# Channel order between two convolutions, chosen so that seven copies of all partitions replace 28 copies of 32

## The chip, the cores and the metric

The program runs on one core of one Trainium2 chip. Its time is the device time of one execution in microseconds (us). Five engines work beside each other: TensorE (PE, its weight loads PEld), VectorE (DVE), ScalarE (ACT), GpSimd (POOL), and SyncE (SP), which here does little but issue DMA copies. Each has a queue of its own that is worked off in order; they wait for each other by semaphores. SBUF has 128 partitions; a tile is written here as partitions x elements.

## The reference

Layer 0 is a residual block of 32 parallel bottleneck paths (P=32, D=4, C=256) over eight images of 56 x 56 x 256; layer 1 is a linear attention and a mixture of eight experts, top two, on the same 25,088 tokens.

```python
def _path(x, w1, b1, g1, be1, m1, v1, w2, b2, g2, be2, m2, v2, w3, b3, g3, be3, m3, v3):
    h = jnp.einsum('nhwc,cd->nhwd', x, w1) + b1                 # 256 -> 4, conv1
    h = jax.nn.relu(_bn(h, g1, be1, m1, v1))
    h = conv_general_dilated(h, w2, (1, 1), 'SAME') + b2        # 3 x 3, 4 -> 4, conv2
    h = jax.nn.relu(_bn(h, g2, be2, m2, v2))
    h = jnp.einsum('nhwd,dc->nhwc', h, w3) + b3                 # 4 -> 256, conv3
    return jax.nn.relu(_bn(h, g3, be3, m3, v3))
x = relu(sum of the 32 paths + x)
t = x + attention(layernorm(x));  t = t + moe(layernorm(t))
```

The 32 paths of four channels make 128 rows, one for each SBUF partition, after conv1 and after conv2.

## The kernel before

The tokens are cut into S = 56 chunks of 448 (eight image rows). A loop over slots (L1462) works on several chunks at once: in slot s, conv3 of chunk s, conv1 of chunk s+2, the copies R and conv2 of chunk s+1, the end of chunk s-1 (store, head statistics), attention of chunk s-8, and the tiles of the experts that are known by then. The `places` table (L1402) gives every step a place between 0 and 1 in its slot, and `issue` (L1430) sorts the steps by it; so PE, ACT and DVE run in this written order. SP and POOL are not among the ordered engines (L72): the scheduler sets their order. Slots before attention starts use the places marked "alone".

The path of a chunk through the first layer:

- conv1 (`conv1_steps`, L240): 128 rows of products, scaled and put by ACT into `h1` (L263), a whole image of 58 x 58 with a border, 128 partitions.
- `spread_taps` (L274): conv2 needs, on partitions 32 dx to 32 dx + 31, the 32 rows of a group g shifted by dx = 0, 1, 2. So R is 96 x 4 x 580, and each of the 4 groups x 3 shifts is one DMA copy of 32 partitions, 12 in all (L284), on SP; for chunk 0 a third of them are on ACT's queue.
- conv2 (`conv2_steps`, L290): for each of three dy, four products, one for each group, with 96 x 32 weights `W2t` (L298); ACT makes `h2` (L307).
- `halves` (L310): DVE splits h2 into hi and lo (L315, L316). conv3 wants, on partitions 4i + v, row i of quarter ab, hi for even v and lo for odd v: `hl` is 128 x 4 x 448. Each of 4 quarters x 4 values of v is one copy of 32 partitions, 16 in all (L321); for chunk 0 half are on ACT's queue.
- conv3 (`pair`, L578): 32 steps of two products (L588), which use `hl[rows, ab, :]` with ab = step // 4 % 4; ACT takes the positive part of one (L593), DVE adds the other (L596), and `sum_paths` (L602) sums the four paths of a partition group on PE (L609).

A copy of SP waits, in the built program, for the copy issued eight before it (eight completion semaphores in turn), besides what it needs itself.

Before the loop stands the setup: loads of W1, bn1, bn2 (L92 to L97), twelve copies W2s on ACT's queue (L206), then conv1 of chunks 0 and 1 and R of chunk 0 (L332, L333), the g and bias copies (L177, two each on SP and ACT), `picks` (L345), which move W3 into `W3hl` through PE (L370 to L381), the bias tables (L384 to L404), conv2 of chunk 0 (L405), and the sums of the biases (L407).

Of the kernel before, what the change touches and what calls it, by code (L numbers as in the profile page):

```python
# [8 lines left out]
F32 = mybir.dt.float32  # L9
# [4 lines left out]
ALU = mybir.AluOpType  # L14
AX = mybir.AxisListType
# [10 lines left out]
def kernel(  # L26
# [24 lines left out]
    nc = tc.nc  # L51
    B, N, C = x.shape
    HW = 56
    NP = W3.shape[0]
    D = W3.shape[1]
# [3 lines left out]
    P = 128  # L59
    NF = C // P  # L60
# [5 lines left out]
    NG = P // 32  # L66
# [9 lines left out]
    const = ctx.enter_context(tc.tile_pool(name="const", bufs=1))  # L76
# [7 lines left out]
    def load(s):  # L84
        b, c = divmod(s, NCH)
        X = xin.tile([T, KT, C], F32, tag="xi", name=f"xi_{s}")
        nc.sync.dma_start(
            out=X, in_=x[b, c * CH : (c + 1) * CH, :].rearrange("(k q) c -> q k c", q=T)
        )
        xs_in[s] = X  # L90

    W1s = const.tile([P, NF, P], F32, name="W1s")  # L92
    nc.sync.dma_start(out=W1s, in_=W1.rearrange("(f c) m -> c f m", c=P))
    bn1s = const.tile([P, 5], F32, name="bn1s")
    nc.sync.dma_start(out=bn1s, in_=bn1)
    bn2s = const.tile([P, 5], F32, name="bn2s")
    nc.sync.dma_start(out=bn2s, in_=bn2)  # L97
    load(0)


    ident = const.tile([P, P], F32, name="ident")
# [45 lines left out]
    GP = NP // NG  # L147
    W2t = const.tile([3 * 32, NG, 3, 32], F32, name="W2t")
# [3 lines left out]
    NPL = 4  # L152
    NQ = NP // (2 * NPL)
# [3 lines left out]
    sumb = const.tile([P, NF, 1], F32, name="sumb")  # L157
# [1 line left out]
    nc.vector.tensor_reduce(  # L159
        gather, ident.rearrange("q (p c) -> q c p", c=32), AX.X, ALU.add  # L160
    )
    xtp = ctx.enter_context(tc.tile_pool(name="xtp", bufs=4))
    taps = ctx.enter_context(tc.tile_pool(name="taps", bufs=1))
    split = ctx.enter_context(tc.tile_pool(name="split", bufs=1))
    hlp = ctx.enter_context(tc.tile_pool(name="hlp", bufs=2))
    setup_pool = tc.tile_pool(name="setup", bufs=1)
    setup = setup_pool.__enter__()


    CQ = C // 4  # L170
# [28 lines left out]
    path32 = setup.tile([P, GP, D], F32, name="path32")  # L199
# [3 lines left out]
    W2s = setup.tile([3 * 32, NG, 3, D], F32, name="W2s")  # L203
    for dx in range(3):
        for g in range(NG):
            nc.scalar.dma_start(  # L206
                out=W2s[32 * dx : 32 * dx + 32, g],
                in_=W2[32 * g : 32 * g + 32].rearrange(
                    "q (dy dx o) -> dx q dy o", dy=3, dx=3
                )[dx],  # L210
            )
    for g in range(NG):
        for dy in range(3):
            nc.vector.tensor_tensor(
                W2t[:, g, dy, :].rearrange("q (p o) -> q p o", o=D),
                path32[: 3 * 32],
                W2s[:, g, dy, None, :].to_broadcast([3 * 32, GP, D]),
                ALU.mult,
            )

# [50 lines left out]
    TL = (ROWS + 2) * W58  # L271
    tapped = {}

    def spread_taps(s):  # L274

        b, c = divmod(s, NCH)
        R = taps.tile([3 * 32, NG, TL], F32, tag="R", name=f"R_{s}")
        flat = h1.rearrange("p r w -> p (r w)")
        r0 = c * ROWS * W58
        for g in range(NG):  # L280
            for dx in range(3):
                n = TL - dx
                queue = nc.scalar if s == 0 and dx == 1 else nc.sync
                queue.dma_start(  # L284
                    out=R[32 * dx : 32 * dx + 32, g, :n],
                    in_=flat[32 * g : 32 * g + 32, r0 + dx : r0 + dx + n],
                )
        tapped[s] = R

    def conv2_steps(s):  # L290
        ps = []

        def taps_of(dy):
            if dy == 0:
                ps.append(ps_mm.tile([P, 512], F32, tag="mm", name=f"c2_{s}"))
            R = tapped[s]
            for g in range(NG):
                nc.tensor.matmul(  # L298
                    ps[0][32 * g : 32 * g + 32, :CH],
                    W2t[:, g, dy, :],  # L300
                    R[:, g, :].rearrange("q (r w) -> q r w", w=W58)[:, dy : dy + ROWS, :HW],
                    start=(dy == 0), stop=(dy == 2),
                )
            if dy == 2:
                del tapped[s]
                h2 = split.tile([P, CH], F32, tag="h2", name=f"h2_{s}")
                nc.scalar.activation(h2, ps[0][:, :CH], AF.Relu, bias=sh2, scale=sc2)  # L307
                h2s[s] = h2

        def halves():  # L310

            h2 = h2s[s]
            hi = split.tile([P, CH], F32R, tag="hi", name=f"hi_{s}")
            lo = split.tile([P, CH], F32R, tag="lo", name=f"lo_{s}")
            nc.vector.tensor_copy(hi, h2)  # L315
            nc.vector.tensor_tensor(lo, h2, hi.bitcast(F32), ALU.subtract)  # L316
            hl = hlp.tile([P, NQ, CH], F32R, tag="hl", name=f"hl_{s}")
            for ab in range(NQ):
                for v, part in enumerate((hi, lo, hi, lo)):
                    queue = nc.scalar if s == 0 and v % 2 else nc.sync  # L320
                    queue.dma_start(  # L321
                        out=hl[v : P : 4, ab, :].bitcast(F32),
                        in_=part[32 * ab : 32 * ab + 32, :].bitcast(F32),
                    )
            h2s[s] = hl

        return [
            (0.8, lambda: taps_of(0)), (0.8, lambda: taps_of(1)), (0.8, lambda: taps_of(2)),
            (0.8, halves),
        ]  # L330

    all_of(conv1_steps(0), conv1_steps(1))  # L332
    spread_taps(0)  # L333


# [9 lines left out]
    picks = setup.tile([P, 2, NQ, P], F32, name="picks")  # L345
    nc.gpsimd.memset(picks, 0.0)
    for part in range(2):
        nc.vector.tensor_copy(
            picks[:, part].rearrange("q a (i v h) -> q (a i) v h", v=2, h=2)[:, :, part, :],
            ident[:, :, None].to_broadcast([P, P, 2]),  # L350
        )

    own = setup.tile([P, P // 16, 16], F32, name="own")
    group_mask(own, P // 16, 16, 1.0)
# [15 lines left out]
    for ab in range(NQ):  # L370
# [12 lines left out]

    pmod = setup.tile([NP, NPL], F32, name="pmod")  # L384
    nc.vector.tensor_reduce(
        pmod, ident[:NP, :NP].rearrange("q (g p) -> q p g", p=NPL), AX.X, ALU.add
    )
    pdiv = setup.tile([NP, NP // NPL], F32, name="pdiv")
    nc.vector.tensor_reduce(
        pdiv, ident[:NP, :NP].rearrange("q (g p) -> q g p", p=NPL), AX.X, ALU.add  # L390
    )
    b4 = setup.tile([NP, NCG, NPL, 32], F32, name="b4")
    for pl in range(NPL):
# [13 lines left out]
    for f in range(NF):  # L407
        tp = ps_mm.tile([P, 512], F32, tag="mm", name=f"tp_sb_{f}")
        nc.tensor.transpose(tp[:, :NP], bias3[:, f * P : (f + 1) * P], ident[:NP, :NP])
        b3T = setup.tile([P, NP], F32, name=f"b3T_{f}")  # L410
        nc.scalar.copy(b3T, tp[:, :NP])
        sub = setup.tile([P, NQ, NPL], F32, name=f"sub_{f}")
        nc.vector.tensor_copy(
            sub, b3T.rearrange("q (a r n) -> q a r n", r=2, n=NPL)[:, :, 1, :]
        )
        nc.vector.tensor_reduce(
            sumb[:, f, :], sub.rearrange("q a n -> q (a n)"), AX.X, ALU.add
        )
    setup_pool.__exit__(None, None, None)

    spill = ctx.enter_context(
# [116 lines left out]
    for e in range(M):  # L538
# [6 lines left out]
        out=below, in_=below, compare_op=ALU.is_ge, fill=0.0, base=-1,  # L545
# [8 lines left out]
        out=earlier, in_=earlier, compare_op=ALU.is_ge, fill=0.0, base=-1,  # L554
# [905 lines left out]
    r, upto = -1, -2  # L1460
    waiting, left = [], []
    for s in range(S + A + 1):  # L1462
        a = s - A
# [6 lines left out]
        if is_chunk(s + 1):  # L1470
            work_of.extend(at("taps" + era, [(0.0, lambda: spread_taps(s + 1))]))
            work_of.extend(at("conv2" + era, conv2_steps(s + 1)))
# [105 lines left out]
```

## Time and profile before

| | us |
|---|---|
| median of three runs | 3262.89 |
| lowest, highest | 3259.10, 3267.65 |
| the profiled execution | 3247.72 |
| its span | 3246.0 |
| PE busy | 2939.6 |
| DVE busy | 2222.5 |
| ACT busy | 1918.3 |
| POOL busy | 1900.8 |
| R copies, SP | 668 of 72 KB |
| hl copies, SP | 888 of 56 KB |

The mean granted TensorE clock was 0.96. Durations below come from the profiled execution, which was 15 us shorter than the median. The views used are: the page (busy shares and the chain of work that ended last), the windows (busy time of each engine in a stretch), the waits (who waited for whom), and the timeline (instructions in order of time: start, length, engine, line, operation, tiles, count, and in brackets the idle time before it and what ended it). A DMA copy in a timeline has the time that its queue needed to issue it, not that of the transfer. "SPq" and "ACTq" are these queues, "PEldq" is PE's.

### The profile page before, as it was taken

The numbers are of one execution on the slowest core, as the hardware profiler recorded it, in microseconds if no ns is written. First come the engines' busy times: TensorE is split into PE (matmuls) and PEld (weight loads), VectorE is DVE, ScalarE is ACT, GpSimd is POOL, SyncE is SP. The second block draws the span as 40 slices with busy tenths as digits, with TensorE's granted clock in tenths as the row PEclk, the third lists the DMA queues.
The fourth block names the chain that finished last, engine by engine and source line by source line (L and its number), as shares of the span: only waits on it lengthen the run. The fifth ranks groups of instructions, "written<-read, shape, count | busy, mean of one in ns | idle before, by whom it ended". The sixth has DMA issues, their size and how long they took to land.

```text
span 3246.0 us, 55293 instructions
## 1 busy us (share of the span) xinstructions
PE 2939.6 (91%) x16677; PEld 1679.8 (52%) x16677; DVE 2222.5 (68%) x5881; ACT 1918.3 (59%) x3827; POOL 1900.8 (59%) x1372
## 2 busy tenths in 40 slices
PE   5999888788999989999899999999999998888798
PEld 2444344343454545455455555555554545777687
DVE  3778877787878687776877787877778775434210
ACT  2676665556666666566666666566666655444345
POOL 3223354445556665746656665656765666777677
PEclk7999998998999999999999999999999999999899
DMA  6432344445666766666666666667576656898897
GB/s 149 131 112 81 107 137 129 115 123 155 166 163 161 186 161 178 165 175 185 169 172 169 188 165 175 176 164 195 156 191 157 181 157 178 199 248 212 196 225 174
DMA packets 341480, 537.71 MB, mean 166 GB/s; under 512 B 59952, under 2 KB 251584, under 8 KB 341184
## 3 DMA queue, kind: packets, MB, share of 16 engines
q1 hardware_dynamic: 257088, 429.93, 45.5%
q0 software_dynamic: 81984, 103.45, 17.2%
q8 instruction: 134, 2.20, 0.3%
q14 instruction: 162, 1.33, 0.1%
q10 hardware_dynamic: 2112, 0.81, 0.1%
HBM read 248.01 MB, written 192.55 MB: 136 GB/s over the span
## 4 chain that ended last, share of the span: by engine, by line
PE 51%; POOL 13%; DVE 11%; issue 8%; DMA 4%; ACT 3%; SPq 0%; POOLq 0%; DVEq 0%; ACTq 0%
PE c L588 9%; PE su L609 9%; PE ph L1321 8%; POOL hsd L720 7%; PE py L1341 7%; PE at L874 5%; DVE r L596 4%; PE kv L748 3%; DMA out_dram<-y,index 3%; POOL out_dram L1359 3%; POOL regions L1065 2%; ACT r L593 2%; PE c L260 2%; PE te L1279 2%; PE py L1337 2%
## 5 line engine op out<-in xcount | busy, mean ns | idle before, releaser
L596 DVE SCALAR_TENSOR_TENSOR r<-c,nb,r 128x448 f32<-128x448 f32 x1792 | 1128.2, 676 | 424.7 <-ACT r L593 379.5
L593 ACT ACTIVATE r<-c,b3t 128x448 f32<-128x448 f32 x1792 | 1038.8, 634 | 346.9 <-PE c L588 342.9
L1359 POOL DMA_INDIRECT out_dram<-y,index x420 | 661.0, 1574 | 329.8 <-ACT y L1345 201.0
L588 PE MATMUL c<-hl,W3hl 64*128 64x448 f32 x3584 | 698.3, 429 | 57.2 <-ACT r L593 25.7
L1065 POOL DMA_INDIRECT regions<-pay,rrowi x448 | 430.7, 961 | 350.5 <-PE c L588 247.4
L609 PE MATMUL su<-r,gather 128*32 128x448 f32 x3584 | 565.3, 571 | 41.6 <-DVE r L596 41.5
L588 PEld LDWEIGHTS c<-hl,W3hl 64*128 64x128 f32 x3584 | 329.2, 189 | 527.4 <-issue 231.4
L1321 PE MATMUL ph<-eT,w 128*128 128x256 f32 x1680 | 463.1, 407 | 42.0 <-DVE r L596 22.6
L1345 ACT ACTIVATE y<-py,g 128x256 f32<-128x256 f32 x420 | 195.9, 475 | 405.5 <-PE py L1341 301.3
L1341 PE MATMUL py<-w,hT 128*128 128x256 f32 x1680 | 434.4, 383 | 0.0
L1321 PEld LDWEIGHTS ph<-eT,w 128*128 128x128 f32 x1680 | 305.6, 197 | 178.1 <-issue 42.9
L720 POOL TENSOR_TENSOR hsd<-hsd,half 112x36 f32<-112x36 f32 x56 | 346.6, 6189 | 84.8 <-DVE hsd L719 84.6
L1325 ACT ACTIVATE hT<-ph,w 128x256 f32<-128x256 f32 x420 | 197.8, 478 | 243.5 <-PE ph L1321 161.9
L1341 PEld LDWEIGHTS py<-w,hT 128*128 128x128 f32 x1680 | 293.2, 192 | 28.4
L682 POOL TENSOR_TENSOR norm<-t,hmean 112x512 f32<-112x512 f32 x112 | 126.8, 1259 | 241.4 <-PE c L588 112.9
L874 PE MATMUL at<-tab,tT 128*112 128x272 f32 x896 | 260.3, 414 | 8.0 <-ACT r L593 6.9
L609 PEld LDWEIGHTS su<-r,gather 128*32 128x32 f32 x3584 | 100.8, 109 | 245.2 <-DVE r L596 129.3
L1337 PE MATMUL py<-b2hl,own 128*128 128x256 f32 x420 | 178.5, 425 | 15.7 <-ACT y L1345 7.6
L874 PEld LDWEIGHTS at<-tab,tT 128*112 128x112 f32 x896 | 148.3, 180 | 82.7 <-ACT r L593 17.3
L1010 POOL TENSOR_TENSOR rq<-ebase,rq 112x8 f32<-112x8 f32 (+1 forms) x32 | 52.6, 1645 | 207.4 <-DVE rq L1009 207.4
L1283 ACT COPY eT<-te 128x512 f32<-128x512 f32 x210 | 123.8, 590 | 65.6 <-PE te L1279 63.8
L1279 PE MATMUL te<-ident,rows 128*128 128x128 f32 x840 | 135.1, 285 | 24.2 <-ACT y L1345 23.6
(255 smaller groups left out, 3222.2 us busy)
## 6 DMA issues: line engine op xcount, KB each, us to landing
w<-Wd SPq DMA_DIRECT2D x210, 513.0 KB
rows<-regions SPq DMA_DIRECT2D x210, 259.0 KB
xi<-in_x_dram SPq DMA_DIRECT2D x56, 448.0 KB
hl<-hi SPq DMA_DIRECT2D x448, 56.0 KB
tTs<-u SPq DMA_DIRECT2D x56, 448.0 KB
ts<-t SPq DMA_DIRECT2D x56, 448.0 KB
tT<-tTs SPq DMA_DIRECT2D x56, 448.0 KB
X<-ts SPq DMA_DIRECT2D x56, 448.0 KB
```

The costliest lines, as they stand in the source:

```text
L588: product = nc.tensor.matmul(tiles[g][:, :CH], W3hl[rows, ab, cg, :], hl[rows, ab, :], start=True, stop=True)
L593: nc.scalar.activation(r, tiles[0][:, :CH], AF.Relu, bias=b3t[:, cg, 2 * ab : 2 * ab + 1])
L596: nc.vector.scalar_tensor_tensor(r, tiles[1][:, :CH], nb3[:, cg, 2 * ab + 1 : 2 * ab + 2], r, op0=ALU.max, op1=ALU.add,)
L609: nc.tensor.matmul(ps[32 * c4 : 32 * c4 + 32, :CH], gather, unit.pop((s, 4 * u + c4)), start=(ab == 0), stop=(ab == NQ - 1),)
L720: nc.gpsimd.tensor_tensor(sd, sd, half[:T, :].rearrange("q (k h) -> q k h", k=KT), ALU.pow)
L874: nc.tensor.matmul(ps, tT[:, f, k * T : (k + 1) * T], tables_of[b][:, f, :], start=(f == 0), stop=(f == NF - 1),)
L1065: ins = nc.gpsimd.indirect_dma_start(out=regions[n], out_offset=bass.IndirectOffsetOnAxis(ap=v["row_i"][:, (m - group[0]) * KT + k, n : n ...
L1279: nc.tensor.transpose(tp[:, f, h * P : (h + 1) * P], z[:, h, f * P : (f + 1) * P], ident)
L1321: nc.tensor.matmul(ps, w[:, f * C + hf * P : f * C + (hf + 1) * P], eT[:, f, :], start=(f == 0), stop=(f == NF - 1),)
L1337: nc.tensor.matmul(ps, own.to_broadcast([P, P]), b2hl, start=True, stop=False)
L1341: nc.tensor.matmul(ps, hT[:, f, h * P : (h + 1) * P], w[:, (NF + f) * C : (NF + f + 1) * C], start=False, stop=(f == NF - 1),)
L1359: ins = nc.gpsimd.indirect_dma_start(out=out_rows, out_offset=at, in_=y[:, h, :], in_offset=None, compute_op=ALU.add, **partial,).ins
```

## The change

The 128 rows after conv1 are numbered so that partition 4i + g, not 32g + i, holds row i of group g, and the rows after conv2 so that a quarter ab of hl lies on every fourth run of the partitions. A copy then takes all 128 partitions: three copies for R (one for each dx) and four for hl (one for each v), seven in place of 28. The bytes are the same. Of chunk 0, one R copy and two hl copies are on ACT's queue.

```diff
+    W1r = setup.tile([P, NF, P], F32, name="W1r")
+    nc.sync.dma_start(out=W1r, in_=W1.rearrange("(f c) m -> c f m", c=P))
+    nc.sync.dma_start(out=bn1s, in_=bn1.rearrange("(g i) k -> i g k", g=NG))
+    for g in range(NG):
+        nc.scalar.dma_start(
+            out=bn2s[32 * g : 32 * g + 32],
+            in_=bn2[32 * g : 32 * g + 32].rearrange("(a e) k -> e a k", a=4),
+        )
     W1s = const.tile([P, NF, P], F32, name="W1s")
-    nc.sync.dma_start(out=W1s, in_=W1.rearrange("(f c) m -> c f m", c=P))
-    nc.sync.dma_start(out=bn1s, in_=bn1)
-    nc.sync.dma_start(out=bn2s, in_=bn2)
+    for f in range(NF):
+        nc.vector.tensor_copy(
+            W1s[:, f, :].rearrange("c (i g) -> c g i", g=NG),
+            W1r[:, f, :].rearrange("c (g i) -> c g i", g=NG),
+        )
...
-        for g in range(NG):
-            for dx in range(3):
-                n = TL - dx
-                queue = nc.scalar if s == 0 and dx == 1 else nc.sync
-                queue.dma_start(
-                    out=R[32 * dx : 32 * dx + 32, g, :n],
-                    in_=flat[32 * g : 32 * g + 32, r0 + dx : r0 + dx + n],
-                )
+        for dx in range(3):
+            n = TL - dx
+            queue = nc.scalar if s == 0 and dx == 1 else nc.sync
+            queue.dma_start(
+                out=R[32 * dx : 32 * dx + 32, :, :n], in_=flat[:, r0 + dx : r0 + dx + n]
+            )
...
-            for ab in range(NQ):
-                for v, part in enumerate((hi, lo, hi, lo)):
-                    queue = nc.scalar if s == 0 and v % 2 else nc.sync
-                    queue.dma_start(
-                        out=hl[v : P : 4, ab, :].bitcast(F32),
-                        in_=part[32 * ab : 32 * ab + 32, :].bitcast(F32),
-                    )
+            for v, part in enumerate((hi, lo, hi, lo)):
+                queue = nc.scalar if s == 0 and v % 2 else nc.sync
+                queue.dma_start(out=hl[v : P : 4, :, :].bitcast(F32), in_=part.bitcast(F32))
...
-        nc.vector.tensor_copy(
-            picks[:, part].rearrange("q a (i v h) -> q (a i) v h", v=2, h=2)[:, :, part, :],
-            ident[:, :, None].to_broadcast([P, P, 2]),
-        )
+        for a in range(NQ):
+            nc.vector.tensor_copy(
+                picks[:, part, a].rearrange("q (i v h) -> q i v h", v=2, h=2)[:, :, part, :]
+                .rearrange("q (g e) h -> q g e h", g=NG),
+                ident.rearrange("q (g a e) -> q a g e", g=NG, a=NQ)[:, a, :, :, None]
+                .to_broadcast([P, NG, 2 * D, 2]),
+            )
...
-        sub = setup.tile([P, NQ, NPL], F32, name=f"sub_{f}")
-        nc.vector.tensor_copy(
-            sub, b3T.rearrange("q (a r n) -> q a r n", r=2, n=NPL)[:, :, 1, :]
-        )
-        nc.vector.tensor_reduce(
-            sumb[:, f, :], sub.rearrange("q a n -> q (a n)"), AX.X, ALU.add
-        )
+        nc.vector.tensor_reduce(sumb[:, f, :], b3T[:, NP // 2 :], AX.X, ALU.add)
```

The rest follows the new numbering: the columns of each 96 x 32 block of W2t are written in another order, and the two reductions behind pmod and pdiv read the identity in another order (over two axes). Five pools (xtp, taps, split, hlp, setup) are opened ahead of these loads. The places, the steps and all products stay as they were.

More of the change, by code (lines that the diff above doesn't have):

```diff
@@ L90, in load @@
         xs_in[s] = X
-    W1s = const.tile([P, NF, P], F32, name="W1s")
-    nc.sync.dma_start(out=W1s, in_=W1.rearrange("(f c) m -> c f m", c=P))
-    bn1s = const.tile([P, 5], F32, name="bn1s")
-    nc.sync.dma_start(out=bn1s, in_=bn1)
-    bn2s = const.tile([P, 5], F32, name="bn2s")
-    nc.sync.dma_start(out=bn2s, in_=bn2)
+    xtp = ctx.enter_context(tc.tile_pool(name="xtp", bufs=4))
+    taps = ctx.enter_context(tc.tile_pool(name="taps", bufs=1))
+    split = ctx.enter_context(tc.tile_pool(name="split", bufs=1))
+    hlp = ctx.enter_context(tc.tile_pool(name="hlp", bufs=2))
+    setup_pool = tc.tile_pool(name="setup", bufs=1)
+    setup = setup_pool.__enter__()
+    W1r = setup.tile([P, NF, P], F32, name="W1r")
+    nc.sync.dma_start(out=W1r, in_=W1.rearrange("(f c) m -> c f m", c=P))
+    bn1s = const.tile([P, 5], F32, name="bn1s")
+    nc.sync.dma_start(out=bn1s, in_=bn1.rearrange("(g i) k -> i g k", g=NG))
+    bn2s = const.tile([P, 5], F32, name="bn2s")
+    for g in range(NG):
[3 more added lines that the diff above has]
+        )
+    W1s = const.tile([P, NF, P], F32, name="W1s")
+    for f in range(NF):
[3 more added lines that the diff above has]
+        )
     load(0)
@@ L161 @@
     )
[L162 to L167, printed above, removed]
     CQ = C // 4
@@ L214 @@
             nc.vector.tensor_tensor(
-                W2t[:, g, dy, :].rearrange("q (p o) -> q p o", o=D),
-                path32[: 3 * 32],
-                W2s[:, g, dy, None, :].to_broadcast([3 * 32, GP, D]),
+                W2t[:, g, dy, :].rearrange("q (b o a) -> q a b o", b=2, o=D),
+                path32[: 3 * 32].rearrange("q (a b) o -> q a b o", b=2),
+                W2s[:, g, dy, None, None, :].to_broadcast([3 * 32, GP // 2, 2, D]),
                 ALU.mult,
@@ L385 @@
     nc.vector.tensor_reduce(
-        pmod, ident[:NP, :NP].rearrange("q (g p) -> q p g", p=NPL), AX.X, ALU.add
+        pmod.rearrange("q (s b) -> q s b", b=2),
+        ident[:NP, :NP].rearrange("q (r s a b) -> q s b r a", r=2, s=2, b=2), AX.XY, ALU.add,
     )
@@ L389 @@
     nc.vector.tensor_reduce(
-        pdiv, ident[:NP, :NP].rearrange("q (g p) -> q g p", p=NPL), AX.X, ALU.add
+        pdiv.rearrange("q (a r) -> q a r", r=2),
+        ident[:NP, :NP].rearrange("q (r s a b) -> q a r s b", r=2, s=2, b=2), AX.XY, ALU.add,
     )
```

## The prediction

> **What bounds the kernel now.** I read the page first (engine shares, chain, groups), then the busy times by stage, then who waits for whom, then SP's and ScalarE's timelines around the copies concerned.
>
> ```profile
> span 3246.0 us, 55293 instructions
> ...
> PE 2939.6 (91%) x16677; PEld 1679.8 (52%) x16677; DVE 2222.5 (68%) x5881; ACT 1918.3 (59%) x3827; POOL 1900.8 (59%) x1372
> ...
> PE 51%; POOL 13%; DVE 11%; issue 8%; DMA 4%; ACT 3%; SPq 0%; POOLq 0%; DVEq 0%; ACTq 0%
> ```
> TensorE is busy for 91% of the span and for half of the chain that ended last; SP's queue has 0% of that chain. By stage (columns: window, then busy us and count of PE, PEld, DVE, ACT, POOL, then clock, DMA share, GB/s):
>
> ```profile
> 0.00:60.00 60.00, 26.75 (x99) 15.76 (x99) 15.35 (x49) 5.75 (x9) 25.25 (x94) 0.77 0.66 142
> 60.00:340.00 280.00, 260.55 (x1516) 113.49 (x1516) 219.39 (x432) 187.75 (x336) 71.68 (x35) 0.98 0.41 113
> ...
> 600.00:2700.00 2100.00, 1963.22 (x11409) 1055.45 (x11410) 1619.24 (x4096) 1314.82 (x2607) 1287.14 (x881) 0.97 0.63 168
> ```
> From 60 us to 2700 us PE is 93% busy; only the head, 0 to 60 us, is held by setup and transfers (PE 45%). The copies concerned run from 24 to 2660 us; the last 550 us have none.
>
> A middle slot on SP (start, length, queue, line, copy):
>
> ```profile
> 1258.75 0.51 SPq L321 DMA_DIRECT2D hl<-hi  x1
> 1259.41 0.50 SPq L321 DMA_DIRECT2D hl<-lo  x1
> ...
> 1268.88 0.59 SPq L321 DMA_DIRECT2D hl<-lo  x1
> ...
> 1277.29 0.35 SPq L649 DMA_DIRECT2D tTs<-u  x1
> 1278.11 7.57 SPq L284 DMA_DIRECT2D R<-h  x12
> ```
> The sixteen hl copies hold SP for 10.7 us here (10.1 in most slots, 0.64 each), the twelve R copies for 7.5. But does anyone wait for them? After the head, in the list of waits from 60 to 2700 us, no PE wait names an R or hl copy, and no engine waits for w, rows, X or tT there for more than 3 us in all. The only place where a copy of this change holds an engine is the head, on ScalarE:
>
> ```profile
> 23.55 3.40 ACTq L284 DMA_DIRECT2D R<-h  x4
> 27.04 1.42 ACTq L181 DMA_DIRECT2D g<-g3q  x2
> 28.56 1.21 ACTq L181 DMA_DIRECT2D bias<-b3q  x2
> 29.81 0.26 ACT L363 COPY spread<-tp_mask 32x128 f32<-32x128 f32 x1 [6.33 <-DMA g<-g3q]
> ...
> 53.92 7.26 ACTq L321 DMA_DIRECT2D hl<-lo  x8
> 61.22 0.27 ACT L411 COPY b3T<-tp_sb 128x32 f32<-128x32 f32 x2 [12.91 <-DMA hl<-lo]
> ...
> 62.34 1.16 ACT L593 ACTIVATE r<-c,b3t 128x448 f32<-128x448 f32 x2
> ```
> ScalarE issues eight hl copies from 53.92 to 61.18 and only then starts the first conv3 result (62.34), though the first product was there at 57.7.
>
> [...]
>
> **Part by part.**
> *SP in a slot.* 28 copies become 7: 21 x 0.64 = 13.4 us of SP per slot, 55 slots. The bytes are the same. What stands behind them on SP (out<-X, w, xi behind hl; ts, tT, rows behind R) leaves up to 10 us sooner. Nobody waits for it, so 0. The new copies have 128 rows; other 128-row copies (tTs, tT) issue in 0.33 to 0.35 us, so I take 0.6 each; the bound is four times that, which would leave SP as it is.
>
> *R.* Counting R's packets (2312 to 2320 bytes) in the trace, the last one ended 1.4 us or more before the first conv2 product in every slot, and that product followed the one before it without a gap in most. Earlier R: 0.
>
> *hl, the part that can cost.* Today the first conv3 product of a slot waits only for the four copies of its quarter (ab=0); afterwards it waits for all four copies, four times the bytes. Packets of 1792 bytes: in slots 1 to 7 the first quarter ends 3.5 us after the first issue (0.7 to 1.5 us before use), the last quarter 11.2 us after, and the first product follows 4.3 to 5.0 us after the issue. From slot 8 on the room after the first quarter is 6 us or more. New landing: the fourth copy leaves 3 x 0.64 = 1.9 us after the first; a large copy's first packet comes 1.1 us after its issue and a tTs copy (459 KB) ends 2.1 us later, 0.22 MB/us; 4 x 229 KB = 917 KB then take 4.2 us, 5.3 in all; at the hl packets' own 74 ns (32 per engine, 2.4 us) it is about 4. I take 0.15 us late in 7 slots, +1; bounds 0 and, if the whole burst lands no sooner than today, (11.2-5.0) x 7 = 43.
>
> *Waits on PE.* conv2's weight loads carry extra wait instructions:
>
> ```profile
> L298 PEldq EVENT_SEMAPHORE x256: 51/51/51, 41.0 to 2641.4; - x128
> ...
>   issue: 57.4, 220
> ```
> They go for groups 1 to 3, since one wait for three copies covers all four groups; the same holds for the second to fourth quarters of L588. PE's queue runs ahead, so most lie under earlier products; the 57 us of "issue" are pacing (the 24 products take 2.46 us either way, PE is busy). Where a load at L298 followed such a wait at once with PE empty, it was 8 times, 1.5 us together. I take -2; bounds 0 and -27 (half of that idle).
>
> *Head.* Removed: three of four R copies on ScalarE (3 x 0.85 = 2.5 us), which stand before the g and bias copies, these before spread, tp_g, W3hl and conv2 of chunk 0. Added: four bn2s copies ahead of W2s on ScalarE's queue (W2s: 12 in 8.52 us, so 4 x 0.71 = 2.8 us); they delay the first xT copy from 10.66 to 13.5, which is hidden, since the second transposes wait for xi until 18.04. If xi came earlier they would show. In the built program both first Wd copies stand ahead of that xi; before, it was one: 256 KB at 0.22 MB/us, +1.2 us. Two W1s reorders on DVE and eight picks copies for two (1.93 us) lie under the same wait and under the wait for g; the reductions and the two sub copies that go are 0.2 us each. Net of this part about -1. Then hl: ScalarE's eight copies become two (7.26 to about 1.8 us). SP reaches hl at 52.02 after pad and Wd traffic that is not shortened; I take 51. The other two leave ScalarE by 54.7, all has landed near 56, and r starts near 57 instead of 62.34: -5.4 for the whole head, bounds -2 and -9.
>
> *Sum:* -5.4 -2 +1 = -6.4. The profiled execution took 3247.7 us (span 3246.0), so 3241.3; it lies 15 us under the median of the runs, 3262.9, and the same difference gives 3256. All of it would be a step at the start; the slots that follow keep their length.
>
> **Rivals.** *B, the slots gain too:* shorter queues and fewer waits take 0.2 to 0.6 us from each of 55 slots, 20 us with the head's 6: 3237. For it: SP holds 17.6 us of copies in a slot of some 50 us, and SP's order moves. Against: no engine is shown waiting for what SP brings. *C, slower:* the place is the first conv3 product of slots 1 to 7, the price what the four hl copies land after 5.0 us, times 7, since PE has nothing in reserve there. It eats the head's gain at 0.9 us each, and is over 0.3% slower from 2.3 us each (landing at 7.3 us, 917 KB at under 150 GB/s); at 4 us it is +28 -7, 3284. Against: the DMA share there is 0.41. *D, it doesn't do what it says:* if a copy of 128 rows issues in 2.4 us, SP and ScalarE save nothing: 3263. tTs speaks against it; I count it with the first case.
>
> **Numbers.** First case (head only, D in its edge) 0.54, 3246 to 3266; B 0.32, 3226 to 3246; C 0.14. About 0.3%, 9.8 us, is what a measurement tells from no change. Faster: 0.15 of the first and 0.31 of B, 0.46. Same: 0.37, 0.01 and 0.03, 0.41. Slower: 0.02 and 0.11, 0.13. Time 3256, the first case; range 3230 to 3274, which leaves out B's far end and most of C.
>
> **What would show it.** SP: hl near 2.4 us and R near 1.9 us per slot. ScalarE: r at 57 rather than 62. Slots 1 to 7 still 33.5 us long (between conv2 starts): right; longer, with a gap ahead of the first L588 product: C. Conv2 starts 6 us earlier at 600 us, and 6 us earlier at 2600 us: the first case; more at 2600: B. Wrong if the new copies take over 1 us each to issue, or if 917 KB take over 6 us.

## The result and the profile after

| | before | after |
|---|---|---|
| median of the runs on one chip, us | 3260.99 (3258.52 to 3267.65) | 3242.39 (3239.81 to 3252.06) |
| ratio, 95% interval | | 0.9945 (0.9919 to 0.9971) |
| the same two again, in a second session, us | 3255.12 (3250.11 to 3263.56) | 3240.35 (3232.95 to 3246.89) |
| ratio, 95% interval | | 0.995 (0.9935 to 0.9965) |
| the profiled execution, us | 3247.72 | 3252.06 |

The kernel became 0.5% faster, 15 to 19 us; 6.4 us had been forecast. The time lies in the range, and the sign is right. The two profiled executions stand the other way round, which is a first lesson: single executions of one kernel differ by 10 us here, so a change of 15 us has to be read from places, not from two spans.

The page of the changed kernel first.

```profile
span 3250.3 us, 53680 instructions
...
PE 2947.0 (91%) x16677; PEld 1672.9 (51%) x16677; DVE 2222.2 (68%) x5887; ACT 1923.3 (59%) x3827; POOL 1900.3 (58%) x1372
```

The engines do what they did; 1613 instructions are gone (55293 before), 1176 of them copies (21 x 56). The chain of waits of this execution breaks off after a few per cent of the span; that of a second execution gives TensorE 51%, as before. By stage (window, then busy us and count of PE, PEld, DVE, ACT, POOL, clock, DMA share, GB/s):

```profile
0.00:60.00 60.00, 24.05 (x97) 13.82 (x97) 18.10 (x57) 5.76 (x11) 25.07 (x94) 0.79 0.75 142
60.00:340.00 280.00, 257.65 (x1496) 110.38 (x1497) 217.44 (x422) 185.68 (x332) 71.68 (x35) 0.97 0.42 111
600.00:2700.00 2100.00, 1966.61 (x11406) 1056.04 (x11405) 1618.42 (x4097) 1316.67 (x2609) 1286.52 (x882) 0.97 0.64 168
```

In the head TensorE has done less by 60 us than before (24.05 us instead of 26.75), and the DMA share rose from 0.66 to 0.75: the head did not get shorter. In the long stretch PE is 3 us busier in the same time. SP's timeline around the copies (start, length, queue, line, copy):

```profile
1258.92 0.56 SPq L333 DMA_DIRECT2D hl<-hi  x1
1259.58 0.54 SPq L333 DMA_DIRECT2D hl<-lo  x1
...
1260.83 0.60 SPq L333 DMA_DIRECT2D hl<-lo  x1
...
1277.46 0.34 SPq L657 DMA_DIRECT2D tTs<-u  x1
1278.28 2.07 SPq L298 DMA_DIRECT2D R<-h  x3
```

hl holds SP for 2.5 us (10.7 before), R for 2.1 (7.5 before). ScalarE in the head:

```profile
25.73 0.62 ACTq L298 DMA_DIRECT2D R<-h  x1
26.45 1.62 ACTq L196 DMA_DIRECT2D g<-g3q  x2
...
57.55 2.30 ACTq L333 DMA_DIRECT2D hl<-lo  x2
...
65.05 1.16 ACT L601 ACTIVATE r<-c,b3t 128x448 f32<-128x448 f32 x2 [4.01 <-issue]
```

Two hl copies, 2.3 us instead of 7.3; but they leave at 57.55 and r starts at 65.05, later than the 62.34 of before. And the waits ahead of conv2's weight loads:

```profile
L311 PEldq EVENT_SEMAPHORE  x99: 51/51/51, 46.8 to 2641.3; - x99
...
  issue: 65.8, 255
```

99 wait instructions instead of 256, and no less "issue" (57.4 before).

To place the rest, the trace was cut at the first conv2 product of each slot; a slot has here the number of the chunk whose conv2 opens it. Each row below gives the kernels with 16 hl copies (before, before again, R part only), then those with four (after, after again, hl part only), in us:

| | 16 copies | 4 copies |
|---|---|---|
| start of conv2 of chunk 1 | 81.0, 84.4, 84.9 | 84.0, 85.4, 83.4 |
| slots 1 to 7, sum | 233.3, 233.3, 233.3 | 233.0, 232.9, 233.3 |
| slots 8 to 13 | 252.7, 252.4, 253.6 | 252.4, 251.7, 250.6 |
| slots 14 to 18 | 231.5, 235.6, 233.9 | 228.7, 228.7, 230.3 |
| slots 23, 30, 44, 51, sum | 207.8, 207.6, 207.6 | 202.9, 202.8, 204.4 |
| the other slots from 19 to 53 | 1585.3, 1592.3, 1585.5 | 1591.7, 1588.7, 1585.9 |

Two rows stand apart from the scatter: four single slots, 1.2 us each, and slots 14 to 18, about 4.4 us. (With hl alone, slot 30 stays at 51.3 us.) The spans of these six executions differ by only 7 us on average, 3252.0 against 3245.0, so they hold half of what the medians show. The experiments take these rows, and the head.

### The profile page after: what moved, and what is told of

It reads as the page before. It is cut to its first block, busy times and chain, and to the rows that moved or that the text cites. A ratio compares the mean times of both kernels' runs of the same rounds, so it can differ in the third digit from the quotient of the medians.

```text
span 3250.3 us, 53680 instructions
## 1 busy us (share of the span) xinstructions
PE 2947.0 (91%) x16677; PEld 1672.9 (51%) x16677; DVE 2222.2 (68%) x5887; ACT 1923.3 (59%) x3827; POOL 1900.3 (58%) x1372
## 5 line engine op out<-in xcount | busy, mean ns | idle before, releaser
L886 DVE SCALAR_TENSOR_TENSOR X<-at,rs,X 112x256 f32<-112x256 f32 x224 | 106.7, 476 | 80.0 <-PE at L882 36.2
```

## The experiments

Each time is set against the kernel before on the same chip in the same session.

**Which half of the change.** First both kernels again, to see what the measurement tells apart.

> The kernel before, unchanged, against itself. Its profiled execution took 3247.7 us where four timed ones took 3258.5 to 3267.7, and of the changed kernel the four lie between 3239.8 and 3252.1. If the gain of 0.55% is a property of the kernels, the ratio here is 1.000 within 0.002; if it is the spread between executions, ratios of 0.995 or 1.005 turn up here too. The profile is a second look at the head: conv2 of chunk 1 should start at 81 us again, within 1 us.

> The changed kernel, unchanged. Real gain: 0.992 to 0.997 again. Spread between executions: 0.998 to 1.002. The first profile has its conv2 of chunk 1 at 84.0 us, 3 us later than before; if the gain came from the head, as forecast (-5), a second profile must show it at 76 us; if it comes from the slots, the head stays at 84 us and the gain shows between 340 and 2700 us.

Measured: before again 3255.8, ratio 1.000 (0.9991 to 1.0009); after again 3240.35, 0.995 (0.9935 to 0.9965). Conv2 of chunk 1 starts at 84.4 in the second profile of the kernel before, not at 81 within 1 us: the head alone scatters by 3 us.

Then the R half alone, made from the kernel before, with W1 and bn1 in the new order:

```diff
-        for g in range(NG):
-            for dx in range(3):
-                n = TL - dx
...
+        for dx in range(3):
+            n = TL - dx
+            queue = nc.scalar if s == 0 and dx == 1 else nc.sync
+            queue.dma_start(
+                out=R[32 * dx : 32 * dx + 32, :, :n], in_=flat[:, r0 + dx : r0 + dx + n]
+            )
```

> Only the three R copies, with the conv1 order that they need; hl keeps 16 copies. 9 of the 21 copies per slot go. Slots theory, gain in step with the number of copies: 9/21 of 0.55%, ratio 0.9976. If the freed order on SP ahead of conv2 is what counts: 0.995 here and 1.000 for the hl part. Head theory: 0.999 to 1.000, since the hl copies on ScalarE's queue stay.

And the hl half alone, the changed kernel with that part undone (twelve R copies, W1 and bn1 loaded plainly):

> Only the four hl copies; R keeps 12 copies and conv1 its order. 12 of the 21 copies per slot go. Slots theory: 12/21 of 0.55%, ratio 0.9969. Head theory: all of it, 0.9945, and conv2 of chunk 1 at 76 to 79 us in the profile. If the wait of the first conv3 product for all four copies costs, slots 1 to 7 are longer than 33.5 us and the ratio is 1.000 or above.

Measured: R alone 3254.34, ratio 0.9999 (0.999 to 1.0008); hl alone 3244.23, 0.9961 (0.9946 to 0.9976). The gain is that of the hl copies. R's 5.4 us of SP per slot and its 160 wait instructions on TensorE (256 before, 96 in this kernel) are worth nothing that can be measured.

**What happens in slot 23.** The same slot in both kernels, first before: VectorE's timeline (start, length, engine, line, operation, tiles), with GpSimd's and TensorE's lines of the same moment.

```profile
1003.86 0.72 DVE L315 CAST hi<-h 128x448 fp32r<-128x448 f32 x1
1004.61 0.63 DVE L316 TENSOR_TENSOR lo<-h,hi 128x448 fp32r<-128x448 f32 x1
...
1007.81 2.79 DVE L896 SCALAR_TENSOR_TENSOR nm<-mv,rs 112x4 f32<-112x4 f32 x1
1010.52 1.26 DVE L596 SCALAR_TENSOR_TENSOR r<-c,nb,r 128x448 f32<-128x448 f32 x2
```

```profile
1003.27 1.62 POOL L1359 DMA_INDIRECT out_dram<-y,index  x1 [0.20 <-issue]
...
1007.46 1.02 POOL L1065 DMA_INDIRECT regions<-pay,rrowi  x1 [0.20 <-issue]
1008.51 2.06 POOL L738 TENSOR_TENSOR norm<-norm,hinv 112x512 f32<-112x512 f32 x2
```

```profile
1011.24 0.38 PE L1337 MATMUL py<-b2hl,own 128*128 128x256 f32 x1 [1.52 <-DVE r L596]
```

Then after, VectorE, GpSimd and TensorE:

```profile
1003.17 0.39 DVE L328 CAST hi<-h 128x448 fp32r<-128x448 f32 x1
1003.60 0.63 DVE L329 TENSOR_TENSOR lo<-h,hi 128x448 fp32r<-128x448 f32 x1
...
1006.79 0.16 DVE L904 SCALAR_TENSOR_TENSOR nm<-mv,rs 112x4 f32<-112x4 f32 x1
1006.86 1.27 DVE L604 SCALAR_TENSOR_TENSOR r<-c,nb,r 128x448 f32<-128x448 f32 x2
1008.05 2.04 DVE L1213 TENSOR_TENSOR big<-one_hot,code 128x80 f32<-128x80 f32 x1
```

```profile
1002.68 1.62 POOL L1367 DMA_INDIRECT out_dram<-y,index  x1 [0.20 <-issue]
...
1006.87 1.02 POOL L1073 DMA_INDIRECT regions<-pay,rrowi  x1 [0.20 <-issue]
1007.90 2.07 POOL L746 TENSOR_TENSOR norm<-norm,hinv 112x512 f32<-112x512 f32 x2
```

```profile
1008.64 0.39 PE L1345 MATMUL py<-b2hl,own 128*128 128x256 f32 x1
```

nm works on four numbers per partition and takes 0.16 us. Before, it took 2.79 us: it started at 1007.81, 0.35 us after GpSimd had begun an indirect copy, and ended at 1010.60, when the norm behind that copy (1008.51 + 2.06 = 1010.57) was done. After, nm started at 1006.79, 0.08 us ahead of that copy, and is through, and the operation that follows the two r's, `big`, is the one that sits there (2.04 us instead of 0.23). (In slot 44 the long one is `table` in two of the three profiles with 16 copies, 2.70 us.) Both end with the norm: nm lasts over most of the copy and both parts of the norm, `big` from 0.15 us after their start (1007.90) to 0.11 us after their end (1009.98). Not every operation becomes long there: in the kernel before, 50 r's ran wholly beside a part of a norm and took 0.67 us, like the others. What makes the one long and not the other is not shown. In either kernel one VectorE operation takes 2 us or more here (2.79 and 2.04); what changed is which. Before, the two r's stood behind the long one, and TensorE's py waited 1.5 us for them. After, the r's are ahead of it.

VectorE came 0.4 us later before, and lost it at hi: it started 0.1 us later within the slot, behind wait instructions, and took 0.72 us instead of 0.39. It takes over 0.7 in just the slots 23, 30, 44 and 51, in each of the three profiles with 16 copies. In these four slots hi falls beside an indirect copy of GpSimd to out_dram (the first line of the GpSimd views above), and the traces of all runs show what goes with that. A hi that began up to 0.52 us after the start of such a copy, or from 0.92 us on, took 0.38 to 0.39 us; one that began between 0.58 and 0.83 us after it took 0.47 to 0.73 and ended 1.30 to 1.40 us after that start. In the three profiles with 16 copies hi begins 0.58 to 0.59 us after it in the four slots, in those of the changed kernel 0.48 to 0.50. (With hl alone, hi of slot 30 begins 0.83 us after it, takes 0.47, and the slot stays long.) Why hi takes longer there is not shown. So 0.1 us of wait instructions lets hi run into one GpSimd copy, and the 0.4 us that are then missing let nm run into another.

The wait instructions are there because hi and lo have one buffer each: VectorE may not write them until the copies out of them in the slot before are done. Sixteen copies on eight semaphores give 384 such DMA waits in the built program over the 56 chunks, four copies 180. No copy was awaited here: the last packet of slot 22's hl copies had ended at 955.5, 48 us ahead of hi. The instructions alone, 0.02 and 0.05 us each, take the time; the trace has 189 of them ahead of hi and lo, that of the changed kernel 92.

Three kernels test this against SP's shorter queue. In the first, the changed kernel, VectorE is only made late:

```diff
-            nc.vector.tensor_copy(hi, h2)
+            for _ in range(2 if s else 1):
+                nc.vector.tensor_copy(hi, h2)
```

> The changed kernel, but VectorE copies h2 into hi twice in every slot after the first (0.38 us more ahead of lo, about 21 us of VectorE in all; SP's copies are untouched). Theory V (what the four hl copies save is VectorE's waits for the copies of the slot before, ahead of hi and lo: 180 DMA waits instead of 384; being about 0.4 us earlier, VectorE gets a product's r done before GpSimd's normalisation blocks it): slots 23, 30, 44 and 51 go back from 50.1 to about 51.3 us, and most of the gain is lost: ratio 0.998 to 1.000 to the kernel before. Theory S (what saves is SP's queue, 10 us shorter per slot): VectorE has room, the ratio stays at 0.995 to 0.9965 and the four slots at 50.1.

In the second, the kernel before, the same waits are only moved:

```diff
                 ps.append(ps_mm.tile([P, 512], F32, tag="mm", name=f"c2_{s}"))
+                for name in ("hi", "lo"):
+                    t = split.tile([P, CH], F32R, tag=name, name=f"{name}_{s}")
+                    nc.vector.memset(t[:, 0:1].bitcast(F32), 0.0)
+                    ps.append(t)
...
-            hi = split.tile([P, CH], F32R, tag="hi", name=f"hi_{s}")
-            lo = split.tile([P, CH], F32R, tag="lo", name=f"lo_{s}")
+            hi, lo = ps[1:]
```

> The kernel before with all its 28 copies, but the tiles hi and lo are taken at the first step of conv2 and touched there by a memset of one column each, so that VectorE waits for the old hl copies there and not ahead of the cast (384 DMA waits as before, only moved; SP untouched; 0.14 us more VectorE work per slot). Theory V: slots 23, 30, 44 and 51 fall from 51.3 to about 50.1 us, and the time falls by 5 to 12 us, ratio 0.996 to 0.9985. Theory S: nothing changes, ratio 0.999 to 1.001, the four slots at 51.3.

In the third, the kernel before, SP's time is doubled:

```diff
-                    queue.dma_start(
-                        out=hl[v : P : 4, ab, :].bitcast(F32),
-                        in_=part[32 * ab : 32 * ab + 32, :].bitcast(F32),
-                    )
+                    for k in range(2 if s else 1):
+                        n = 16 if s else 32
+                        queue.dma_start(
+                            out=hl[v + 64 * k : 64 * k + 4 * n : 4, ab, :].bitcast(F32),
+                            in_=part[32 * ab + 16 * k : 32 * ab + 16 * k + n, :].bitcast(F32),
+                        )
```

> The kernel before with each hl copy cut in two from the second chunk on: 32 copies of 16 rows, about 20 us of SP per slot instead of 10, the same bytes, and about the same waits on VectorE (359 DMA waits ahead of hi and lo, against 384). Theory S: slower by 10 us or more, ratio 1.003 and up. Theory V: ratio 0.999 to 1.001 and slots 23, 30, 44 and 51 still at 51.3, unless SP becomes so full that something else comes late, which would show as a new wait in the trace.

The lists of waits, TensorE from 800 to 2700 us (tile and line, what it waited for, us in total, times, longest), at py: the kernel before, the changed kernel, hi twice, the waits moved.

```profile
PE py L1337 <- DVE r L596: 6.3, 5, 1.5
```

```profile
PE py L1345 <- DVE r L604: 0.3, 1, 0.3
```

```profile
PE py L1346 <- DVE r L605: 6.3, 5, 1.5
```

```profile
PE py L1340 <- DVE r L599: 0.3, 1, 0.3
```

A delay of 0.4 us on VectorE puts the whole wait back (the four slots: 208.2 us); moving the waits in the kernel before, with its sixteen copies, takes it away (203.6). The times: hi twice 3246.95, ratio 0.9968 (0.9959 to 0.9978); waits moved 3253.33, 0.9989 (0.9979 to 0.9999). So the chain from hi to py is shown in both directions, and its size is what four slots give, 4 to 5 us: a third of the gain, not most of it as theory V had it (0.998 to 1.000 was expected for hi twice, 0.996 to 0.9985 for the waits moved). The time of hi twice holds something else besides: its slots 1 to 7 take 236.3 us, 3.3 more than in the changed kernel.

The 32 copies cost 3316.3, ratio 1.0174 (1.015 to 1.0198): the exception that the expectation left to theory V. Of the 60 us, 51 are in slots 1 to 7 (283.9 instead of 233.3), where TensorE now waits (same view, 115 to 400 us):

```profile
PE c L590 <- DMA hl<-lo: 19.8, 20, 2.5
PE c L298 <- DMA R<-h: 11.5, 14, 1.1
```

In the traces the granted clock is full or half (84 records in the kernel before, 42 of each, all but the last a multiple of 3.4 us long); TensorE ran at half clock for 61 us in these slots, half of which is lost, and for none in the kernel before. SP's 10 us per slot were hidden, and the 20 us that the expectation estimates are not. That tells nothing on the step from 10 to 2.5. Two of the four slots, 30 and 51, became short here (50.1 and 49.9 us): in these hi began 0.51 and 0.49 us after the start of GpSimd's copy, and took 0.39.

**Half of SP's time, all of the waits.** The changed kernel with each hl copy in two halves of the columns has, by the expectation's estimate, half of SP's time of before (5 us per slot, for 10.7), but as many waits on VectorE, and each first product waits for eight copies:

```diff
-            for v, part in enumerate((hi, lo, hi, lo)):
-                queue = nc.scalar if s == 0 and v % 2 else nc.sync
-                queue.dma_start(out=hl[v : P : 4, :, :].bitcast(F32), in_=part.bitcast(F32))
+            w = CH // 2
+            for k in range(2):
+                for v, part in enumerate((hi, lo, hi, lo)):
...
+                        out=hl[v : P : 4, :, k * w : k * w + w].bitcast(F32),
+                        in_=part[:, k * w : k * w + w].bitcast(F32),
```

> The changed kernel with each of the four hl copies cut into two halves of the columns: eight copies, about 5 us of SP per slot instead of 2.5, and as many DMA waits on VectorE ahead of hi and lo as before the change (383). Every conv3 product of the first step now waits for all eight copies, the last of which lands about 6.5 to 7 us after the first issue, while the product is due 5.0 us after it. Theory V (VectorE's waits decide slots 23, 30, 44 and 51): the PE wait ahead of py in slots 19 to 54 goes from 0.7 back to about 6.7 us and the four slots to 51.3 us, though SP is at half of what it was. Rival C of the prediction, here with its price: slots 1 to 7 grow from 33.3 by 1 to 3 us each. Theory B2 (the 1.8 us less PE idle time in slots 14 to 18 comes from the order of the PSUM banks in the built program, which here is that of the changed kernel): PE idle there 35.5 us, not 37.3. Time 3250 to 3270. Theory S alone: four slots at 50.7, halfway.

Measured: 3270.86, ratio 1.0038 (1.0025 to 1.0051). Waits of TensorE at py (800 to 2700 us), and from 115 to 345 us:

```profile
PE py L1350 <- DVE r L609: 6.4, 5, 1.5
```

```profile
PE c L601 <- DMA hl<-lo: 9.8, 5, 2.4
```

The wait at py is back, and the four slots take 207.7 us, though SP is, by that estimate, at half its time: theory V again. And here rival C of the prediction is seen with its price: slots 1 to 7 take 254.2 us, 3 us more each, since the last copy comes after the product is due (8.5 us in all were lost at half clock there, none in the changed kernel).

**Slots 14 to 18.** TensorE's idle time there (gaps between the end of one product and the start of the next, summed) is 37.4, 37.0, 37.7 us with sixteen copies, and 35.4, 35.3, 35.6 with four. It follows neither VectorE's waits (waits moved: 37.3; hi twice: 34.9; eight copies: 35.4) nor R. One part is plain: in two rounds of ranking, rk's first product starts 0.05 us after ScalarE's r with sixteen copies and 0.05 us after VectorE's, 0.26 us earlier, with four. In the built program rk waits for another reader; that it is one of another PSUM bank is the author's guess, which no trace here shows. Why, and whether the waits of each quarter's first product on TensorE do the rest, was not separated. The lengths differ by more than the idle time: all five profiles with sixteen copies have 231.5 us or more there, the seven with eight or four 231.4 or less, and most of that difference is time at half clock. The number of copies alone doesn't order them: the kernel with 32 has 224.7 us there, and 30.7 us of idle time.

**TensorE's clock.** Every timed run lists the mean clock that TensorE was granted, as a share of full clock. The share that was not granted, times the span, is the time lost to it:

| kernel | runs | median granted clock | lost, mean, us |
|---|---|---|---|
| before, three sessions | 27, 39, 19 | 0.957 in each | 140, 140, 142 |
| R alone | 14 | 0.958 | 136 |
| waits moved | 22 | 0.957 | 140 |
| hi twice | 18 | 0.961 | 125 |
| hl alone | 6 | 0.961 | 128 |
| changed, second session | 6 | 0.9625 | 122 |

(The first four runs of the changed kernel list 0.959 each.) The kernels with sixteen copies lose more than those with four. Among the runs of the kernel before, one microsecond more lost goes with 0.35 to 0.58 us more time, so 15 to 18 us less would be worth 5 to 10 us; that is an estimate from these runs. The two tests of the four slots fit it. Hi twice has these slots as long as before and is still 10 us faster, with 15 us less lost; the waits moved have them short and gain 3 us, with as much lost as before. By the profiles the difference lies in slots 8 to 18: on average 45 us lost there in the five with sixteen copies, 36 in the six with four. So the four slots and the clock can together make up the gain. Why TensorE was at full clock for longer with four copies, and whether that is a cause or follows from the shorter idle time, is open.

**The head.** In the changed kernel tp_g waits for g until 35.89 (30.11 before). g is four copies of 8 KB; ScalarE sent its two by 28.07, yet they landed near 35.8, 7.7 us later; before, it was 1.7. The packets show what went in between: from 26 to 34 us a pad, an xi and the R copies, which are now three of 300 KB, sent within 2 us; g's packets of 256 bytes move from 32 us on. (With R alone changed, the first pad leaves at 28.39, and tp_g still starts only at 33.51; so it isn't the pads alone.) SP:

```profile
24.56 0.49 SPq L1256 DMA_DIRECT2D regions<-pad  x1
25.68 1.30 SPq L298 DMA_DIRECT2D R<-h  x2
29.88 0.40 SPq L1256 DMA_DIRECT2D regions<-pad  x1
```

In the kernel before, SP sent eight small R copies until 30.1, and the pads only then. With g and bias on SP they go ahead of R:

```diff
-            queue = nc.sync if q % 2 else nc.scalar
-            queue.dma_start(out=t[:, q * CQ : (q + 1) * CQ], in_=parts_of[q : P : 4, :])
+            nc.sync.dma_start(out=t[:, q * CQ : (q + 1) * CQ], in_=parts_of[q : P : 4, :])
```

> The changed kernel with the g and bias copies of the head all on SP (half of them were on ScalarE's queue, behind its work and beside 265 KB pad transfers that SP sends from 24.8 us on). Theory H (the head is held by g, which lands at 36 to 37 us because the pads are in front of or beside it): tp_g starts at 27 to 29 us, conv2 of chunk 0 at about 40 instead of 48.5 to 49.6, conv2 of chunk 1 at 75 to 78 instead of 84 to 85; time 7 us below the changed kernel, about 3233. Rival: another wait of the head takes its place (R of chunk 0, or hl), and less than 2 us are gained.

TensorE, the changed kernel, then this one:

```profile
35.89 1.19 PE L377 MATMUL tp_g<-g,spread 32*128 32x256 f32 x2 [10.81 <-DMA g<-g3q]
```

```profile
24.73 0.83 PE L376 MATMUL tp_g<-g,spread 32*128 32x256 f32 x2 [2.09 <-DMA g<-g3q]
```

Measured: 3231.57, ratio 0.9915 (0.9895 to 0.9935); conv2 of chunk 1 starts at 76.9. It beats both kernels: it is 25.0 us below the kernel before, the changed kernel was 14.8 below it in another session, so about 10 us of this are the edit's. The same edit in the kernel before:

> The kernel before, with the g and bias copies of the head all on SP, as in e8. In the kernel before the pads come only after R, so g is late by ScalarE's four R copies alone: tp_g from 30.1 to about 26, conv2 of chunk 1 about 3 us earlier, time 3252. If the gain of e8 has nothing to do with what SP sends earlier in the changed kernel, it is 8 us here too.

Measured: 3257.17, ratio 1.0001 (0.9992 to 1.001). Its head is shorter too (conv2 of chunk 1 at 77.8, tp_g at 27.64), but this execution gives it back: slots 8 to 13 take 260.3 us, with 29.0 us lost at half clock there against 15.4 to 18.8 in the other four profiles with sixteen copies. Over all its 14 runs no more is lost than in the kernel before (141 us against 142), so where the head's gain goes in the others is open.

Last, e8 with the bulk copies tied to slots:

```diff
+        def paced(queued):
+            tc.add_manual_dep(queued.ins, pace[0].name, SYNC, reason="not in the head")
...
+            tc.add_manual_dep(ins, pace[0].name, SYNC, reason="not in the head")
             filled(0, ins)
```

> e8 (changed kernel, g and bias on SP), and the copies of the experts' weights and the pads of the first slots each tied to a conv3 product of its slot, so that SP can't send them in the head. Theory H: the xi of chunk 1 lands 3 to 6 us earlier and hl of chunk 0 lands at about 50 instead of 57, so conv2 of chunk 1 starts at 65 to 71 instead of 76.9 and the time is 3222 to 3227. Rival: the bulk copies, 8 MB in slots 1 to 8 instead, delay hl or R there (slots 1 to 7 longer than 33.5 us) and give it back.

Measured: 3234.49, ratio 0.9925 (0.9912 to 0.9938), no better than e8. Conv2 of chunk 1 starts at 75.6, just 1.3 us earlier, and slots 1 to 7 take 234.7 instead of 233.0: the rival. hl of chunk 0 still leaves only at 50, since conv2 of chunk 0 came at 42.2 after a wait for g of 6.7 us; why g is late there was not followed.

## Why the prediction was right or wrong

*SP: 2.4 us for hl, 1.9 for R; right* (2.5 and 2.1). Rival D is out. One hl copy left SP every 0.64 us before; 0.66 us lie between the starts of two of the new ones (1258.92 and 1259.58).

*R earlier costs and brings nothing: right*, 0.9999 for R alone.

*hl lands about 5 us after the first issue, in time: right.* Over slots 1 to 7 all four copies land 3.9 to 4.6 us after it, the product comes at 5.0 (in slot 1 at 4.4, where they land at 4.0), and slots 2 to 7 stay at 33.5. Rival C did not come, and the eight halves show how near it was: 2 us later, and it costs 3 us per slot.

*Head, -5.4: wrong.* The sum let SP reach hl at 51 and ScalarE's copies leave by 54.7; they left at 57.3 and 57.55, and r started at 65.05 instead of 57. The failed step is "Net of this part about -1": it counted instructions on queues, one by one, and let SP's freed time stand empty. It filled with pads and large R copies, behind which g came 6 us later than before. In two profiles each conv2 of chunk 1 starts at 82.7 us on average before and at 84.7 after: +2, no more than the scatter, in place of -5.4. So the main term of the sum had the wrong sign, and that the total came out in the right direction is luck, as far as this sum goes.

*Waits on PE, -2: not told apart from nothing.* R alone takes away 160 of them, and its ratio is 0.9999, with 3 us to either side. And the list was short: the prediction looked for removed waits on TensorE only. The removed waits that are shown to count are VectorE's ahead of hi and lo, for the copies of the slot before: a term that the sum did not have. "Nobody waits for it, so 0", said of what stands behind SP, holds for R; nobody waited for the hl copies in these slots either, and yet their wait instructions made what stands behind VectorE late.

*Rival B, slots gain, 3237: this is what happened*, in size (3242 and 3240), not in form. It is no 0.2 to 0.6 us in each slot, but 1.2 in each of four, some 4.4 in slots 14 to 18, and nothing in slots 1 to 7 and in most others. The argument against it ("no engine is shown waiting for what SP brings") was true and did not bear on it.

*The sum as measured,* from the averages of the table's two columns: head +1, four slots -4.3, slots 14 to 18 -4.4, slots 8 to 13 -1.3; the other rows scatter by more than they differ. That is -9.0, of 15 between the medians and 7 between the spans of these six executions. The four slots are shown by experiment. Of slots 14 to 18 a quarter of a microsecond per round is located, and most of the rest is time at half clock. The prediction has no term for that clock. In single executions this time scatters by more than 10 us: 131.5, 140.4 and 127.7 us lost to it in the three profiles with sixteen copies, 135.8, 132.1 and 130.4 with four (3.4 us at half clock lose 1.7); it takes the runs of a whole session to tell the kernels apart. All records at half clock together lose 4% of the span here (131.5 of 3246.0 us in the kernel before).

## What to carry to other kernels

When copies are merged, count the waits of the engine that next writes their source, not only of the one that reads their target: with a single buffer for each of hi and lo, sixteen copies gave VectorE 384 such waits here and four gave 180, and the wait instructions took 0.02 or 0.05 us each though, in the slot followed, the copies had landed 48 us before. In this kernel a tenth of a microsecond on VectorE, which is busy for 68% of the span, cost nothing in most slots and 1.2 us in each of four; look for slots that have the same length in every profile of one kernel and another in every profile of the other. Compare the granted clock of all runs before a gain of half a per cent is put down to places in the program. And SP's freed issue time did not stay free here: pads and large R copies filled it, and the product that waits for g started 5.8 us later (35.89, 30.11 before). Ask what the queue will send instead, and put small copies that something waits for ahead of it.

## What was not expected of the hardware

- A VectorE operation of 0.16 us took 2.79 us beside an indirect copy and a norm of GpSimd, ending 0.03 us after the norm; in the changed kernel another took 2.04 instead of 0.23.
- A cast of 0.39 us took up to 0.73 when it began 0.58 to 0.83 us after the start of GpSimd's indirect copy to out_dram, and 0.39 when it began 0.1 us sooner.
- A copy of 8 KB needed 7.7 us to land behind pads and R, and 1.7 before.
- Bringing the head forward by 3 to 7 us left the time of the kernel before unchanged, while 7 to 8 us in the changed kernel brought it about 10.
